# Slot distances on GpSimd instead of ScalarE, and the layer-1 bias of two more chunks in ten written by ScalarE: a graph network kernel on one core

## The chip, the cores and the metric

The kernel runs on one core of one Trainium2 chip. The metric is the time of one execution in device microseconds. The kernel before the change takes 575.55 us (median of three runs, 574.04 to 575.84). Its profiled execution spans 573.7 us, at a mean granted TensorE clock of 0.983.

## The reference, cut to what matters

128 graphs of 64 nodes with 128 features each. For every pair of nodes (i, j) a message is made by a three-layer network with layer norms, multiplied by the adjacency (0 or 1), and summed over j; a second network turns the sum and the node's own features into an update.

```python
def _mlp(x, w0, b0, g0, be0, w1, b1, g1, be1, w2, b2):
    h = relu(x @ w0 + b0);  h = _layernorm(h, g0, be0)
    h = relu(h @ w1 + b1);  h = _layernorm(h, g1, be1)
    return h @ w2 + b2

pair_feats = concatenate([f_i, f_j], axis=-1)             # (B, 64, 64, 256)
messages   = _mlp(pair_feats, msg...) * coupling_matrix[..., None]
agg        = sum(messages, axis=2)
updated    = part_feats + _mlp(concatenate([part_feats, agg], axis=-1), upd...)
```

The adjacency is sparse: each entry is set with a chance of 1/16, made symmetric, with the diagonal. So the kernel computes messages for edges alone.

## The kernel before

The graphs are taken in pairs, 128 nodes on 128 partitions. The edges of a graph get `CAP` = 640 slots, in the order of their node i. 64 pairs make 160 **chunks** of 512 slots (`NCHK`), and every ten chunks (`CPB`) form a block of four pairs, whose adjacency is handled together. The edge-level work is one software pipeline: iteration n runs layer 0 of chunk n and layer 1 of chunk n - 8 (`L1` = `QC` + 3 = 8), with everything else hung into it by a table, `at(iteration, place, function, ...)`. Each engine executes its instructions in the order in which the loop emits them. The places are run as follows.

```python
for n in range(last + 1):
    run(n, "a")
    run(n, "m")
    ...
    if 0 <= n - L1 < NCHK:
        layer1(n - L1)
    run(n, "b")
    if n + LEAD < QC or QC <= n < NCHK:
        layer0(n if n >= QC else n + LEAD)
    if n + 1 < QC or QC <= n - 1 < NCHK - 1:
        stats0(n - 1 if n > QC else n + 1)
    run(n, "k")
    if 0 <= n - L1 < NCHK:
        stats1(n - L1)
    for k in ("x", "x1", "x2", "e0", "e1", "e"):
        run(n, k)
```

**Slots.** Node i of a graph owns the slots from `before` + 1 to `cum`, `deg` of them. `slot` holds 1, 3, 5 ... (twice the slot's number less one), and `mid` = `cum` + `before`, so a slot belongs to the node where |slot - mid| < deg. `distance` writes |slot - mid| for 640 slots, `make_tp` compares it with the degree and gives the matrix `tp` of ones and zeros, from which come the selection matrix of layer 0 (through a cast, `node_rows`, and a DMA), the marks of node j (`marks`) and the weights of the sum.

```python
slot = const.tile([P, CAP], F16, name="slot")
nc.gpsimd.iota(slot, pattern=[[2, CAP]], base=1, ...)

def distance(p):
    b, q = divmod(p, PB)
    D[p] = tpp.tile([P, CAP], F16, name="d", bufs=2)
    nc.scalar.activation(D[p], slot, AF.Abs, bias=blocks[b]["mid"][:, q:q + 1], scale=-1.0)

def make_tp(p):
    b, q = divmod(p, PB)
    tp = tpp.tile([P, CAP], F16, name="tp")
    nc.vector.tensor_scalar(tp, D.pop(p), blocks[b]["deg"][:, q:q + 1], None, op0=ALU.is_lt)
    TP[p] = tp
# ... in the schedule, for p > 2, with n = p * 10 // 4:
at(max(n - 7, p - 2), "a", distance, p)
at(max(n - 6, p - 2), "m", make_tp, p)
at(n - 5, "a", node_rows, p)
```

**Layer 0 and its statistics.** `layer0` makes 512 columns of `hps` in PSUM by matmuls with the selection matrix, and ScalarE turns them into h. `stats0` transposes the four tiles of the chunk before into one bank `hT`, from which VectorE takes mean and variance. GpSimd and ScalarE turn those into a deviation `m_sd` per edge, every five chunks.

**Layer 1 and its bias.** The first layer norm is folded into the next weights, so the layer-1 bias of an edge is `b1b` times the edge's own deviation. There are two ways to put it into the bank `z` before the four matmuls of the chunk add to it. Either ScalarE writes it, four activations of 128x128 (`seed`), or TensorE does, by one matmul with the transposed deviations (`sdT`) as weights. There are two `z` banks, used in turn.

```python
def seed(n):
    q, c = divmod(n, QC)
    z_of(n)
    SEEDED.add(n)
    for t in range(CH):
        k = CH * c + t
        nc.scalar.activation(Z[n][:, t, :], W["b1b"], AF.Copy, scale=SR[q][:, k:k + 1])

def layer1(n):
    q, c = divmod(n, QC)
    ps = z_of(n)
    del Z[n]
    h = H.pop(n)
    if n not in SEEDED:
        nc.tensor.matmul(ps, lhsT=SD[q], rhs=W["b1t"][:, CH * c:CH * c + CH, :],
                         start=True, stop=False, skip_group_check=True)      # line 602
    for t in range(CH):
        nc.tensor.matmul(ps[:, t, :], lhsT=h[:, t * P:(t + 1) * P], rhs=W["w1c"],
                         start=False, stop=True, skip_group_check=True)      # line 605
    Y[n] = yp.tile([P, CH, C], F32, name="y")
    nc.scalar.activation(Y[n], ps, AF.Relu)
# ... in the schedule:
for n in range(2, NCHK - L1):
    if n % CPB in (0, 1, 2, 6, 7, 9):
        at(n + L1 - 2, "x", seed, n)
```

So six of ten chunks are seeded by ScalarE, each in the iteration two before its layer 1, and four (3, 4, 5, 8) get their bias from TensorE.

**GpSimd.** Its work in the loop: `place` and `place_out` (the slots of a block), `node_rows`, the small steps from statistics to variances (`square_sum`, `var1_of`), the low part of the deviations, the weights of the sum, and the residual.

Of the kernel before, what the change touches and what calls it, by code (L numbers as in the profile page):

```python
# [9 lines left out]
F32 = mybir.dt.float32  # L10
# [3 lines left out]
AF = mybir.ActivationFunctionType  # L14
ALU = mybir.AluOpType
AX = mybir.AxisListType
PSUM = bass.MemoryType.PSUM

EPS = 1e-5
BIG = 3.0e38  # L20


@with_exitstack
def tile_gnn(
# [40 lines left out]
    nc = tc.nc  # L65
    B, N, C = x.shape
    P = 128
# [6 lines left out]
    CH = 4  # L74
    QC = QT // CH
    NCHK = NQ * QC
    PB = 4
    NB = NP // PB
    CPB = NCHK // NB
# [57 lines left out]
    eps_c = const.tile([P, 1], F32, name="eps_c")  # L137
    nc.vector.memset(eps_c, EPS)
    eps2_c = const.tile([P, 1], F32, name="eps2_c")
# [18 lines left out]
    slot = const.tile([P, CAP], F16, name="slot")  # L158
# [77 lines left out]
    def add_relu(o, ps, sb):  # L236

        nc.vector._custom_dve(TENSOR_ADD_SAT, out=o, in0=ps, in1=sb, s0=BIG, s1=0.0)

    def square_sum(stp, st, n, name, eng=nc.gpsimd):  # L240

        d = stp.tile([P, n], F32, name=name + "_d")
        s = stp.tile([P, n], F32, name=name + "_s")
        m2 = stp.tile([P, n], F32, name=name)
        eng.tensor_tensor(d, st[:, :, 1], st[:, :, 4], op=ALU.subtract)  # L245
        eng.tensor_tensor(s, st[:, :, 2], st[:, :, 5], op=ALU.add)
        eng.tensor_tensor(d, d, d, op=ALU.mult)
        eng.tensor_scalar(d, d, C / 4.0, None, op0=ALU.mult)
        eng.tensor_tensor(m2, d, s, op=ALU.add)
        return m2  # L250
# [7 lines left out]
    def var1_of(stp, st, m20, n, name, eng=nc.gpsimd):  # L258

        v = stp.tile([P, n], F32, name=name + "_v")  # L260
        eng.tensor_scalar(v, m20, EPS, None, op0=ALU.mult)
        m2 = square_sum(stp, st, n, name, eng)
# [22 lines left out]
    def edge_path(es):  # L285
        blkp = es.enter_context(tc.tile_pool(name="blk", bufs=3))
        adp = es.enter_context(tc.tile_pool(name="adp", bufs=2))
# [36 lines left out]
        def at(n, place, fn, *args):  # L324
            plan.setdefault((n, place), []).append((fn, args))

        def run(n, place):
            for fn, args in plan.pop((n, place), ()):
                fn(*args)

        blocks = {b: {} for b in range(NB)}
        TP, S, H, ST0, V0, SD, SH, Y, ST1, Q, OH, WT, YS, MK, D, IR, JR, SR, Z = ({} for _ in range(19))
# [42 lines left out]
        def place(b):  # L375

            blk = blocks[b]
            cum = cumall[:, b * PB:(b + 1) * PB]
            before = adp.tile([P, PB], F32, name="before")
            nc.gpsimd.tensor_tensor(before, cum, blk["deg"], op=ALU.subtract)  # L380
            blk["mid"] = adp.tile([P, PB], F32, name="mid")
            nc.gpsimd.tensor_tensor(blk["mid"], cum, before, op=ALU.add)
            pos = adp.tile([P, PB, N], F32, name="pos")
            nc.gpsimd.tensor_tensor(pos, blk.pop("rk"),
                                    before.unsqueeze(2).to_broadcast([P, PB, N]), op=ALU.add)
            blk["pos"] = pos
# [88 lines left out]
        def distance(p):  # L475
            b, q = divmod(p, PB)
            D[p] = tpp.tile([P, CAP], F16, name="d", bufs=2)
            nc.scalar.activation(D[p], slot, AF.Abs, bias=blocks[b]["mid"][:, q:q + 1], scale=-1.0)  # L478

        def make_tp(p):  # L480

            b, q = divmod(p, PB)
            tp = tpp.tile([P, CAP], F16, name="tp")
            nc.vector.tensor_scalar(tp, D.pop(p), blocks[b]["deg"][:, q:q + 1], None,  # L484
                                    op0=ALU.is_lt)
            TP[p] = tp

        def node_rows(p):
# [89 lines left out]
        def z_of(n):  # L578

            if n not in Z:  # L580
                Z[n] = zbank(n % 2).rearrange("p (t c) -> p t c", t=CH)
            return Z[n]

        def seed(n):

            q, c = divmod(n, QC)
            z_of(n)
            SEEDED.add(n)  # L590
            for t in range(CH):
                k = CH * c + t
                nc.scalar.activation(Z[n][:, t, :], W["b1b"], AF.Copy, scale=SR[q][:, k:k + 1])  # L593

# [204 lines left out]
        L1 = QC + 3  # L799
# [29 lines left out]
        for b in reversed(range(NB)):  # L829
            o = b * CPB  # L830
            n = o + QC + SC

            if b < NB - 1:
                t = STEADY if b < NB - 3 else LAST[b - NB + 3]
# [32 lines left out]
        for p in range(NP):  # L867
            n = p * TG * 2 // CH
            if p > 1:
                if p > 2:  # L870
# [3 lines that stand above are left out]
                at(n - 4, "a", stack, p, 0, IR)  # L874
                for k in range(2):
                    at(n - 5 + k, "k", marks, p, k)
                    at(n - 5 + k, "k", compare, p, k)
                at(n - 3, "a", stack, p, 1, JR)
            w = p // 2 * QC + QC + L1 + p % 2
            last = p // 2 == NQ - 1  # L880
            at(w - 4, "a", node_marks, p)
            q, h = divmod(p, 2)
            for g in range(2):
                wait = h + 2 if q == NQ - 3 else h + 1 if q == NQ - 2 else 2 + (2 * h + g + 1) // 2
                at(*((NCHK + L1, "b") if last else (q * QC + QC + L1 + wait, "e1")), weights, p, g)
            at(NCHK + L1 + 1 if last else q * QC + SC - (q >= NQ - 3), "x1", reduce, p)
        for q in range(NQ):
            n = q * QC + QC if q else LEAD
# [12 lines left out]
        for n in range(2, NCHK - L1):  # L901
            if n % CPB in (0, 1, 2, 6, 7, 9):
                at(n + L1 - 2, "x", seed, n)

# [12 lines left out]
        degrees(0)  # L919
        place_first()  # L920
        distance(0)
        place_pair(0)
        make_tp(0)
        place_rest()
        bias_rows()
# [25 lines left out]
        compare_here(0, 0)  # L951
        rows_lo(0, 0, 0, 2)
        distance(1)
        layer0(0)
        compare_here(0, 1)
        make_tp(1)
        distance(2)
        bias_parts()
# [89 lines left out]
    with ExitStack() as es:  # L1048
        es.enter_context(tc.manual_schedule())
        flag = edge_path(es)  # L1050
# [160 lines left out]
```

## Time and profile before

| engine | busy, us | share of the span | instructions |
|---|---|---|---|
| TensorE, matmul | 549.3 | 96% | 5303 |
| TensorE, weight load | 515.0 | 90% | 5303 |
| VectorE | 479.8 | 84% | 1944 |
| ScalarE | 476.3 | 83% | 1149 |
| GpSimd | 339.6 | 59% | 898 |

The profile calls TensorE PE, its weight load PEld, VectorE DVE, ScalarE ACT and GpSimd POOL. A row of the groups gives the source line, the engine, the operation, the tiles it writes and reads, its shape and count, then busy time and mean duration in ns, then the engine's idle time just before it. A row of the timeline gives start and length in us, then the same names, and in square brackets how long the engine had been idle and whom it waited for. Neighbouring instructions of one kind are merged into one row with a count. Instructions of ScalarE overlap a little, so the time from one start to the next is shorter than a duration; durations of GpSimd are rough.

The operations that the change touches, by their rows in the groups:

| operation | engine | count | mean, ns |
|---|---|---|---|
| distance `d`, 128x640 float16 | ScalarE | 64 | 823 |
| `make_tp`, 128x640 float16 | VectorE | 64 | 385 |
| seed of `z`, 128x128 | ScalarE | 360 | 371 |
| bias matmul of `z`, 80x512 | TensorE | 70 | 484 |

### The profile page before, as it was taken

What the parts mean: (1) busy time and instruction counts of PE and PEld (TensorE: products, weight loads), DVE (VectorE), ACT (ScalarE), POOL (GpSimd) and SP (SyncE); (2) the same over time, 40 slices, a digit from 0 to 9 for tenths busy, and PEclk for the clock granted to TensorE, in tenths of its full rate; (3) what the DMA queues carried; (4) which work ended last, traced back from release to release, by engine and by line L of the source; (5) the groups of instructions that cost most, each with busy time, mean ns of one, the idle gap of its engine ahead of it and who ended that gap; (6) DMA issues with size and microseconds to landing.
All of it is one profiled execution on the core that took longest, in us unless ns stands there. A gap on an engine that the chain in (4) does not pass through costs nothing. (4 is left out here: it accounts for less than half of the span.)

```text
span 573.7 us, 15753 instructions
## 1 busy us (share of the span) xinstructions
PE 549.3 (96%) x5303; PEld 515.0 (90%) x5303; DVE 479.8 (84%) x1944; ACT 476.3 (83%) x1149; POOL 339.6 (59%) x898
## 2 busy tenths in 40 slices
PE   6899899999999999999999999999999999989894
PEld 4687889999999999999999999999999999979883
DVE  5768788997979899797989889798989979786686
ACT  6788979998988889898888989898888989875434
POOL 3435566665657676575757666565767656545342
PEclk7899999999999999999999999999999999998998
DMA  4464645555465545457574545546475464531201
GB/s 101 102 146 114 133 105 133 101 134 111 103 153 111 134 96 142 113 113 128 125 134 110 138 109 130 105 111 154 102 128 108 125 115 109 114 93 30 35 21 41
DMA packets 90769, 63.21 MB, mean 110 GB/s; under 512 B 57398, under 2 KB 74812, under 8 KB 90684
## 3 DMA queue, kind: packets, MB, share of 16 engines
q1 hardware_dynamic: 90396, 62.03, 49.1%
q8 instruction: 43, 0.70, 0.5%
q14 instruction: 42, 0.34, 0.2%
q10 hardware_dynamic: 288, 0.13, 0.1%
HBM read 6.82 MB, written 4.19 MB: 19 GB/s over the span
## 5 line engine op out<-in xcount | busy, mean ns | idle before, releaser
L548 DVE BATCH_NORM_STATS2 st<-hT 128x6 f32<-128x128 f32 x640 | 141.9, 284 | 36.4 <-PE hT L544 34.8
L605 PE MATMUL z<-w1c,h 128*128 128x128 f32 x1280 | 172.2, 277 | 0.0
L605 PEld LDWEIGHTS z<-w1c,h 128*128 128x128 f32 x1280 | 161.2, 192 | 8.0 <-issue 5.1
L593 ACT ACTIVATE z<-b1b,m_sd 128x128 f32<-128x128 f32 x360 | 133.6, 371 | 8.7
L615 DVE BATCH_NORM_STATS2 st<-y 128x6 f32<-128x128 f32 x640 | 137.5, 277 | 2.7 <-ACT y L608 1.4
L608 ACT ACTIVATE y<-z 128x512 f32<-128x512 f32 x160 | 94.5, 591 | 26.2 <-PE z L605 24.5
L538 ACT ACTIVATE h<-hps,b0c 128x512 f32<-128x512 f32 x160 | 109.4, 684 | 3.6 <-PE hps L535 3.3
L544 PE MATMUL hT<-ident,h 128*128 128x128 f32 x640 | 98.2, 276 | 1.5 <-DVE st L548 1.5
L678 POOL TENSOR_TENSOR w<-oh,m_q 128x320 f32<-128x320 f16 x126 | 91.9, 741 | 9.9 <-PE hT L544 5.3
L535 PE MATMUL hps<-s,abl 128*128 128x512 f32 (+3 forms) x256 | 93.2, 376 | 3.7 <-ACT h L538 2.8
L544 PEld LDWEIGHTS hT<-ident,h 128*128 128x128 f32 x640 | 76.7, 142 | 12.0 <-ACT h L538 1.3
L493 POOL CAST i<-tp 128x640 fp32r<-128x640 f16 x58 | 41.6, 718 | 68.0 <-DVE tp L484 49.1
L535 PE MATMUL hps<-s,abh 128*128 128x512 f32 (+3 forms) x256 | 79.5, 329 | 0.0
L691 PE MATMUL ys<-y,w 128*64 128x128 f32 x1280 | 76.9, 275 | 0.0
L691 PEld LDWEIGHTS ys<-y,w 128*64 128x64 f32 x1280 | 69.2, 137 | 4.2 <-issue 3.6
L245 POOL TENSOR_TENSOR m_d<-st 128x20 f32<-128x20 f32 x62 | 16.3, 263 | 88.4 <-DVE st L548 76.7
L517 DVE TENSOR_TENSOR j<-mk,cmpt 128x320 fp32r<-128x320 f32 x124 | 58.6, 473 | 1.2 <-PE mk L509 1.2
L535 PEld LDWEIGHTS hps<-s,abl 128*128 128x128 f32 x256 | 50.0, 195 | 6.2 <-ACT h L538 4.5
L478 ACT ACTIVATE d<-slot,mid 128x640 f16<-128x640 f16 x64 | 52.7, 823 | 0.0
L535 PEld LDWEIGHTS hps<-s,abh 128*128 128x128 f32 x256 | 50.3, 197 | 0.0
L469 DVE TENSOR_TENSOR abl<-mu,abh 128x512 fp32r<-128x512 f32 (+1 forms) x33 | 22.3, 675 | 31.9 <-ACT abh L463 31.7
L509 PE MATMUL mk<-tp,posall 128*128 128x320 f16 x126 | 38.0, 301 | 1.1 <-DVE tp L484 0.9
(226 smaller groups left out, 978.2 us busy)
## 6 DMA issues: line engine op xcount, KB each, us to landing
s<-i SPq DMA_DIRECT2D x124, 160.0 KB, 2.7
s<-j SPq DMA_DIRECT2D x124, 160.0 KB, 2.6
xn<-in_x_dram SPq DMA_DIRECT2D x15, 256.0 KB, 3.6
out_dram<-uo SPq DMA_DIRECT2D x15, 256.0 KB, 2.4
an<-in_adj_dram SPq DMA_DIRECT2D x16, 128.0 KB, 2.7
oh<-tp SPq DMA_TRANSPOSE x64, 3.6
xn<-in_x_dram SPq DMA_DIRECT2D x2, 128.0 KB
out_dram<-uo SPq DMA_DIRECT2D x2, 128.0 KB, 2.6
```

Of the source, the lines that this page charges most:

```text
L478: nc.scalar.activation(D[p], slot, AF.Abs, bias=blocks[b]["mid"][:, q:q + 1], scale=-1.0)
L517: nc.vector.tensor_tensor(JR[p][:, c], MK.pop((p, k))[:, 0:HC], cmpt[:, c], op=ALU.is_equal)
L535: nc.tensor.matmul(ps[:, c:c + w], lhsT=ab[:, g % 4, :], rhs=s, start=(k == 0), stop=(k == 1))
L538: nc.scalar.activation(H[n], ps, AF.Relu, bias=b0c)
L544: nc.tensor.transpose(ps[:, t, :], H[n][:, t * P:(t + 1) * P], ident)
L548: nc.vector.bn_stats(ST0[q][:, CH * c + t, :], ps[:, t, :])
L593: nc.scalar.activation(Z[n][:, t, :], W["b1b"], AF.Copy, scale=SR[q][:, k:k + 1])
L605: nc.tensor.matmul(ps[:, t, :], lhsT=h[:, t * P:(t + 1) * P], rhs=W["w1c"], start=False, stop=True, skip_group_check=True)
L608: nc.scalar.activation(Y[n], ps, AF.Relu)
L615: nc.vector.bn_stats(ST1[q][:, CH * c + t, :], Y[n][:, t, :])
L678: (nc.vector if p == NP - 2 else nc.gpsimd).tensor_tensor(WT[p][:, :, g, :], OH[p][:, :, g * N:(g + 1) * N], Q[q][:, k:k + TG].unsqueeze(2 ...
L691: nc.tensor.matmul(YS[b][g * N:(g + 1) * N, k, :], lhsT=w[:, t, g, :], rhs=y, start=(t == 0), stop=(t == TG - 1))
```

## The change: what it does and what it is for

**Distances on GpSimd.** From the second block on, `distance` is one GpSimd instruction with two operations, (slot x scale) + shift, written as float16. `scale` is 1 / (2 deg), with deg taken as at least 0.5, and `shift` is 1536 - mid x scale. In float16 the numbers around 1536 are whole, so the result rounds to exactly 1536 where |slot - mid| is below deg, and to another number elsewhere. `make_tp` then asks for equality with the constant 1536 in place of a comparison with the degree of the partition. The block's `place` computes `scale` and `shift` once for its four pairs: two small operations on VectorE and three on GpSimd where there was one. The first block keeps the old way. This frees ScalarE of 60 of its 64 distances.

**More seeds on ScalarE.** From the second block on, chunks 5 and 8 of each block are seeded by ScalarE too, and TensorE's bias matmul for them goes. Their seeds are spread over two iterations: of chunk 5 two tiles in the iteration two before its layer 1, two in the one just before; of chunk 8 three and one. Eight of ten chunks are now seeded, and 3 and 4 keep the matmul.

```diff
+TIE = 1536.0
@@ place(b)
-            blk["mid"] = adp.tile([P, PB], F32, name="mid")
-            nc.gpsimd.tensor_tensor(blk["mid"], cum, before, op=ALU.add)
+            half = adp.tile([P, PB], F32, name="half")
+            nc.vector.tensor_scalar(half, blk["deg"], 0.5, 2.0, op0=ALU.max, op1=ALU.mult)
+            blk["scale"] = adp.tile([P, PB], F32, name="scale")
+            nc.vector.reciprocal(blk["scale"], half)
+            mid = adp.tile([P, PB], F32, name="mid")
+            nc.gpsimd.tensor_tensor(mid, cum, before, op=ALU.add)
+            nc.gpsimd.tensor_tensor(mid, mid, blk["scale"], op=ALU.mult)
+            blk["shift"] = adp.tile([P, PB], F32, name="shift")
+            nc.gpsimd.tensor_scalar(blk["shift"], mid, -1.0, TIE, op0=ALU.mult, op1=ALU.add)
@@ distance(p)
-            nc.scalar.activation(D[p], slot, AF.Abs, bias=blocks[b]["mid"][:, q:q + 1], scale=-1.0)
+            if b == 0:
+                nc.scalar.activation(D[p], slot, AF.Abs, bias=blocks[b]["mid"][:, q:q + 1],
+                                     scale=-1.0)
+                return
+            nc.gpsimd.tensor_scalar(D[p], slot, blocks[b]["scale"][:, q:q + 1],
+                                    blocks[b]["shift"][:, q:q + 1], op0=ALU.mult, op1=ALU.add)
@@ make_tp(p)
-            nc.vector.tensor_scalar(tp, D.pop(p), blocks[b]["deg"][:, q:q + 1], None,
-                                    op0=ALU.is_lt)
+            if b == 0:
+                nc.vector.tensor_scalar(tp, D.pop(p), blocks[b]["deg"][:, q:q + 1], None,
+                                        op0=ALU.is_lt)
+            else:
+                nc.vector.tensor_scalar(tp, D.pop(p), TIE, None, op0=ALU.is_equal)
@@ seed(n)
-        def seed(n):
+        def seed(n, t0=0, t1=CH):
...
-            for t in range(CH):
+            for t in range(t0, t1):
@@ schedule of the seeds
             if n % CPB in (0, 1, 2, 6, 7, 9):
                 at(n + L1 - 2, "x", seed, n)
+            elif n > CPB and n % CPB in {5: 2, 8: 3}:
+                k = {5: 2, 8: 3}[n % CPB]
+                at(n + L1 - 2, "x", seed, n, 0, k)
+                at(n + L1 - 1, "x", seed, n, k, CH)
```

## The prediction, on record before the changed kernel was run

> **What bounds the kernel now.** I read the windows view first: the busy time of each engine in one block of ten chunks from the middle of the run, and in the block before it.
>
> ```profile
> 273.95:306.80 32.85, 32.85 (x331) 31.39 (x329) 28.94 (x120) 29.32 (x72) 21.23 (x58) 1.00 0.58 121
> 241.10:273.95 32.85, 32.85 (x332) 31.40 (x329) 28.94 (x120) 29.32 (x72) 21.21 (x58) 1.00 0.63 121
> ```
>
> The columns are the length of the stretch, then TensorE, weight load, VectorE, ScalarE and GpSimd busy, then the granted clock, the DMA share and GB/s. A block takes 32.85 us and TensorE is busy for all of it, twice in a row. So the bound is TensorE's instruction stream, in order and without a gap; ScalarE has 3.5 us per block to spare, GpSimd 11.6. Two consequences: an instruction taken from TensorE shortens the block by its slot, and any new wait on TensorE lengthens it by the whole wait, since nothing there is idle to absorb it.
>
> Next, the page's groups, for what the change touches:
>
> ```profile
> L593 ACT ACTIVATE z<-b1b,m_sd 128x128 f32<-128x128 f32 x360 | 133.6, 371 | 8.7
> L478 ACT ACTIVATE d<-slot,mid 128x640 f16<-128x640 f16 x64 | 52.7, 823 | 0.0
> ```
>
> Then the timeline, at the two places where the change takes the bias matmul (line 602) away. I name iterations by number modulo ten: an iteration n runs layer 1 of chunk n-8, so chunk 5 of a block is multiplied in iteration 3 and chunk 8 in iteration 6. TensorE and ScalarE from iteration 2 into 3:
>
> ```profile
> 273.35 0.29 PE L535 MATMUL hps<-s,abh 128*128 128x256 f32 x1
> 273.48 0.60 PE L544 MATMUL hT<-ident,h 128*128 128x128 f32 x4
> 273.92 0.30 PE L509 MATMUL mk<-tp,posall 128*128 128x320 f16 x1
> 273.95 0.50 PE L602 MATMUL z<-b1t,sdT 80*128 80x512 f32 x1
> ...
> 271.73 0.68 ACT L773 ACTIVATE usdb<-bu1b,um_sd 128x128 f32<-128x128 f32 x2
> 272.32 0.25 ACT L573 CAST sdT<-ma 80x128 fp32r<-80x128 f32 x1
> 273.19 0.60 ACT L608 ACTIVATE y<-z 128x512 f32<-128x512 f32 x1 [0.63 <-PE z L605]
> 273.69 0.68 ACT L538 ACTIVATE h<-hps,b0c 128x512 f32<-128x512 f32 x1
> 274.27 1.58 ACT L593 ACTIVATE z<-b1b,m_sd 128x128 f32<-128x128 f32 x4
> ```
>
> The reader sees that the bias matmul of chunk 5 starts at 273.95, right behind the marks; its four layer-1 matmuls follow at 274.29, so its slot is 0.34 us. ScalarE starts h at 273.69, as soon as the last hps matmul is out, and its next instruction at 274.27. The other place, iterations 4 to 6:
>
> ```profile
> 281.35 0.70 ACT L538 ACTIVATE h<-hps,b0c 128x512 f32<-128x512 f32 x1
> 282.13 0.58 ACT L741 COPY ysumT<-ma 128x512 f32<-128x512 f32 x1
> 282.61 0.83 ACT L478 ACTIVATE d<-slot,mid 128x640 f16<-128x640 f16 x1
> 283.34 0.30 ACT L269 ACTIVATE m_sq<-m_v,eps_c 128x20 f32<-128x20 f32 x1
> 283.54 0.59 ACT L608 ACTIVATE y<-z 128x512 f32<-128x512 f32 x1
> 284.02 0.69 ACT L538 ACTIVATE h<-hps,b0c 128x512 f32<-128x512 f32 x1
> ...
> 284.22 0.47 PE L602 MATMUL z<-b1t,sdT 80*128 80x512 f32 x1
> ```
>
> Here the layer-1 matmuls follow at 284.53, a slot of 0.31 us. ScalarE runs back to back from 282.13 on.
>
> **What the Trainium skill says.** "ScalarE: Activation LUTs", section "What ACT_TABLE_LOAD costs", gives an activation with one per-partition pointer 280 ns plus 0.833 ns an element, and lets neighbours overlap by some 93 ns. The trace agrees: 823 ns for 640 elements (813 by the page), with the next instruction 0.73 us after its start (282.61 to 283.34). "PSUM — Partial Sum Buffer", section "PSUM bank collisions raise a hardware error", asks that PSUM be guarded by semaphores per bank, not per address. The trace looks like it: two usdb writes, into SBUF, take 0.68 us, a pace of 0.30, but four seeds into one bank take 1.58, a pace of (1.58 - 0.37)/3 = 0.40, as if each waited for the one before. And in iteration 5 the four transposes of hT run from 281.06 to 281.66, the first of them (272 ns) done by 281.34, yet the statistics of the first start at 281.69. I therefore take it that layer 1 of a chunk can't start before the last seed of its bank is written, even where its first quarter was ready long before. "GPSIMD Engine Reference", section "Engine selection", calls one-input operations on GpSimd roughly line rate; the cast of 128x640 float16 at 718 ns agrees. "SBUF — State Buffer", section "Who interferes with whom", has GpSimd and a two-port VectorE operation shut each other out; one make_tp of 1094 ns against a median of 369 may be that.
>
> **The change part by part.** 60 of 64 distances leave ScalarE: four per block, 4 x 0.73 = 2.9 us. They sit in iterations 0, 3, 5 and 8. Eight seeds per block come in: 3 x 0.40 + 0.32 for four, 1.53 us, so 3.1 us for two chunks. ScalarE comes out even, at some 29.5 of 32.85 us. The sum is not the point; the place is.
>
> TensorE: chunks 15, 25 ... 145 and 18, 28 ... 148 lose the bias matmul, 28 in all, worth 0.34 + 0.31 = 0.65 us per block, 14 x 0.65 = 9.1 us. That is the whole possible gain: 575.5 - 9.1 = 566.4.
>
> New wait in iteration 3. Chunk 5's seeds 0 and 1 go into iteration 1, after usdb: ScalarE is there at 272.32 and done with them 0.40 + 0.32 later, 273.04, then sdT (0.16 to the next) until 273.20, so the 0.63 us of idle before y is just filled and h stays at 273.70. Seeds 2 and 3 come after h of iteration 2: 273.70 + 0.57 = 274.27 start, + 0.40 + 0.37 = 275.04 end of the last, + 0.06 for the signal = 275.10. TensorE has nothing between the marks and layer 1, so it is ready at 273.95: it waits 1.15 us to save 0.34. Net + 0.81.
>
> New wait in iteration 6. Chunk 8's seeds 0 to 2 go after h of iteration 4: 281.35 + 0.57 = 281.92, three seeds 2 x 0.40 + 0.32 = 1.13, so 283.05; ysumT 0.48, no distance, m_sq 0.20, y 0.48: h of iteration 5 starts at 284.21 instead of 284.02, and seed 3 ends at 284.21 + 0.57 + 0.37 = 285.15, with the signal 285.21. TensorE is ready at 284.22: it waits 0.99 to save 0.31. Net + 0.68.
>
> GpSimd: four distances per block. No row has two pointer scalars. The trace has a 128x128 multiplication by one pointer scalar at 616 ns (line 648) and a constant one of 128x20 at 258, so a pointer may add some 0.25 us; my estimate is 616 + 512 x 0.83 + 250 = 1.3 us. 5.2 us per block on 21.2 leaves 6 idle. In the GpSimd timeline the four places have room: in iteration 0 it waits 2.4 us for VectorE, in iteration 5 2.6 us; in iterations 3 and 8 it pushes the variance steps back by 1.3 us, which ScalarE wants two iterations later. make_tp on VectorE comes an iteration later too. VectorE's comparison keeps type and size, so its 369 ns; two 128x4 operations per block, about 0.2 us each, lie in its 3.9 us of slack.
>
> Sum: 14 x (0.81 + 0.68) = 14 x 1.49 = 20.9 us. 575.55 + 20.9 = 596.5 us.
>
> **The rivals.** (1) Waits by the seed's own quarter and not by the bank: then matmuls of quarter 0 and 1 start at once, quarter 2 (TensorE there at 274.38) waits for 274.70, quarter 3 for 275.10; layer 1 ends about where it ends now, and chunk 8 behaves alike. Nearly nothing is gained or lost: about 572 to 577. The pace of 0.40 and the statistics' wait speak against it. (2) Seeds in time: if ScalarE, freed of the distances, ran ahead, 566.4. Against it: h can't start before TensorE's hps, whatever ScalarE is spared, and the last seed follows h. (3) GpSimd becomes late: its constant scalar operations of 4 and 20 elements, 223 and 258 ns, differ by 2.2 ns an element; at that slope a distance takes 616 + 512 x 2.2 + 250 = 2.0 us, its block has 29 us of 33, and the deviation chain of iteration 5 starts some 0.7 us late, which delays the transposed deviations on TensorE. The wait in iteration 3 gives it 0.8 us of room, so this would add 0 to 5 us in all. (4) The waits are partly hidden at the start and end, where TensorE idles anyway (the last two of the 14 blocks): 2 or 3 us less.
>
> **Range and chances.** The main term rests on order and on durations that repeat to 10 ns; the open point is whether the bank is the unit of waiting (I give it 0.88) and by how much the restart of TensorE and GpSimd add. Predicted 596.5 us, range 585 to 602. Faster by over 2% 0.05 (even rival 2 stops at 1.6%), within 2% 0.13, slower by over 2% 0.82.
>
> **What would show it.** In the changed trace: line 602 at 42 matmuls; seeds at 472; TensorE waiting for seeds 28 times, about 1.1 us each, in iterations 3 and 6, so 25 to 30 us in the waits; a middle block of about 34.3 us with TensorE busy for some 32.2; distances on GpSimd near 1.3 us; h of iteration 5 about 0.2 us later against y's own matmuls. A block at 32.2 us with no such wait would prove me wrong, as would waits on GpSimd in their place.

## The result, and the profile after

The changed kernel takes 605.39 us (median of four runs, 603.87 to 606.93) against 574.88 us before (four runs, 574.04 to 575.84). The ratio is 1.053, with a 95% interval from 1.0488 to 1.0572. It is slower by 30.5 us, where 21 had been predicted, and lies 3.4 us above the range.

The head of the page, then its groups that answer to those of before:

```profile
span 602.2 us, 15901 instructions
PE 550.9 (91%) x5275; PEld 510.7 (85%) x5275; DVE 484.6 (80%) x1974; ACT 475.1 (79%) x1201; POOL 397.9 (66%) x988
```

```profile
L624 PE MATMUL z<-w1c,h 128*128 128x128 f32 x1280 | 175.5, 280 | 22.6 <-ACT z L612 22.6
L612 ACT ACTIVATE z<-b1b,m_sd 128x128 f32<-128x128 f32 x472 | 173.0, 371 | 10.6
L493 POOL TENSOR_SCALAR d<-slot,scale,shift 128x640 f16<-128x640 f16 x60 | 58.1, 968 | 0.1
L621 PE MATMUL z<-b1t,sdT 80*128 80x512 f32 x42 | 20.2, 480 | 0.0
```

ScalarE's total busy time hardly moved (475.1 against 476.3), as the prediction had it: 112 more seeds, 60 fewer distances. TensorE runs 28 bias matmuls fewer (42), and it now stands idle ahead of the layer-1 matmuls for 22.6 us, waiting for seeds. The same is in the table of waits (engine and tile waiting, for whom; us in total, number of times, longest; at the 28th place, in the last block, TensorE waits 2.83 us for `ysumT` instead):

```profile
PE z L624 <- ACT z L612: 22.6, 27, 1.1
```

And a block of ten chunks, in the windows (the columns are those of the prediction's first fence):

```profile
253.75:288.30 34.55, 32.90 (x329) 31.01 (x326) 29.32 (x121) 29.44 (x76) 25.15 (x63) 1.00 0.51 115
```

A block takes 34.55 us instead of 32.85, and TensorE, busy for all of it before, is idle for 1.65. The two places are the predicted ones. Iteration 2 into 3 in the timeline, ScalarE first and TensorE under it:

```profile
286.66 0.76 ACT L612 ACTIVATE z<-b1b,m_sd 128x128 f32<-128x128 f32 x2
...
288.08 0.68 ACT L557 ACTIVATE h<-hps,b0c 128x512 f32<-128x512 f32 x1
288.65 2.28 ACT L612 ACTIVATE z<-b1b,m_sd 128x128 f32<-128x128 f32 x6
...
288.30 0.30 PE L528 MATMUL mk<-tp,posall 128*128 128x320 f16 x1
289.48 1.16 PE L624 MATMUL z<-w1c,h 128*128 128x128 f32 x8 [0.88 <-ACT z L612]
```

Two seeds of chunk 5 are written from 286.66 on. The other two are the first of the six that start at 288.65, behind h: at a pace of 0.40 us the second of them ends at 288.65 + 0.40 + 0.37 = 289.42. TensorE finishes the marks and then waits until 289.48, although the first quarters had been ready for two microseconds. So layer 1 waits for the last write to the tile `z`; the tile is one bank, and no run here tells bank and tile apart. From the marks to layer 1 it was 0.37 us before and is 1.18 now: + 0.81. Iterations 4 to 6:

```profile
297.22 1.20 ACT L612 ACTIVATE z<-b1b,m_sd 128x128 f32<-128x128 f32 x3
298.35 0.58 ACT L760 COPY ysumT<-ma 128x512 f32<-128x512 f32 x1
298.83 0.31 ACT L270 ACTIVATE m_sq<-m_v,eps_c 128x20 f32<-128x20 f32 x1
299.04 0.58 ACT L627 ACTIVATE y<-z 128x512 f32<-128x512 f32 x1
299.52 0.69 ACT L557 ACTIVATE h<-hps,b0c 128x512 f32<-128x512 f32 x1
300.08 1.07 ACT L612 ACTIVATE z<-b1b,m_sd 128x128 f32<-128x128 f32 x3
...
299.16 0.60 PE L755 MATMUL ma<-ident,uy 128*128 128x128 f32 x4
300.51 1.16 PE L624 MATMUL z<-w1c,h 128*128 128x128 f32 x8 [0.76 <-ACT z L612]
```

The fourth seed of chunk 8 starts at 300.08 and ends 0.37 later, at 300.45; TensorE goes on at 300.51, 0.06 after it. Against the work around it, layer 1 starts 0.69 us later than before.

A second loss lies outside the blocks, at the start. The first layer-1 matmul of the loop starts at 38.89 us, before at 34.80: + 4.1. The span of 28.5 us more is made up of this 4.1, of 23.8 between the first and the last chunk's layer 1 (536.36 us against 512.58), and of 0.6 behind it. The start in the timeline, GpSimd, then ScalarE, then TensorE:

```profile
20.18 0.20 POOL L388 TENSOR_TENSOR mid<-cumall,before 128x4 f32<-128x4 f32 x1
22.66 0.20 POOL L389 TENSOR_TENSOR mid<-mid,scale 128x4 f32<-128x4 f32 x1 [2.28 <-DVE scale L386]
...
25.51 0.88 POOL L493 TENSOR_SCALAR d<-slot,scale,shift 128x640 f16<-128x640 f16 x1
...
29.98 0.31 ACT L256 ACTIVATE m_sd<-m,eps_c 128x20 f32<-128x20 f32 x1 [5.40 <-POOL m L250]
30.45 0.40 ACT L178 ACTIVATE wg<-u,ug1c 128x128 f32<-128x128 f32 x1
...
30.90 0.80 PE L181 MATMUL z<-wg,mean_m 128*128 128x128 f32 x2 [3.14 <-ACT wg L178]
```

It is read as a chain. GpSimd needs the second block's `scale`, and VectorE computes that behind four statistics and a comparison: GpSimd stands for 2.28 us. The position table, the bias table and the first variances (`m`) follow behind it on GpSimd, with a distance in between. So ScalarE waits 5.40 us for `m` (before 1.79), and what stands behind it on ScalarE, `wg` (a folding of weights), comes late too: TensorE waits 3.14 us, where before it had waited 1.59, for an h.

### The profile page after: what moved, and what is told of

Its sections match the earlier page's. It is cut to its first block, busy times and chain, and to the rows that moved or that the text cites. A ratio compares the mean times of both kernels' runs of the same rounds, so it can differ in the third digit from the quotient of the medians.

```text
span 602.2 us, 15901 instructions
## 1 busy us (share of the span) xinstructions
PE 550.9 (91%) x5275; PEld 510.7 (85%) x5275; DVE 484.6 (80%) x1974; ACT 475.1 (79%) x1201; POOL 397.9 (66%) x988
## 5 line engine op out<-in xcount | busy, mean ns | idle before, releaser
L624 PE MATMUL z<-w1c,h 128*128 128x128 f32 x1280 | 175.5, 280 | 22.6 <-ACT z L612 22.6
L624 PEld LDWEIGHTS z<-w1c,h 128*128 128x128 f32 x1280 | 159.4, 192 | 36.9 <-ACT z L612 30.2
L612 ACT ACTIVATE z<-b1b,m_sd 128x128 f32<-128x128 f32 x472 | 173.0, 371 | 10.6
L493 POOL TENSOR_SCALAR d<-slot,scale,shift 128x640 f16<-128x640 f16 x60 | 58.1, 968 | 0.1
L472 ACT CAST abh<-mu 128x512 fp32r<-128x512 f32 (+1 forms) x33 | 18.9, 572 | 45.7 <-PE mu L460 45.7
```

Of the source, the lines that this page charges most:

```text
L493: nc.gpsimd.tensor_scalar(D[p], slot, blocks[b]["scale"][:, q:q + 1], blocks[b]["shift"][:, q:q + 1], op0=ALU.mult, op1=ALU.add)
```

## The experiments

Three theories were on the table. **A**: the 30 us are waits for late seeds, by the bank, in the two places. **B**: a part comes from GpSimd's distances, at the start or in the blocks. **C**: the seeds cost, wherever they are written, because ScalarE has no room. Each ratio is to the kernel before in the same session, where that took 575.6 to 576.3 us. No version leaves out a needed part of the computation.

**The distances alone.** The changed kernel without the new seeds:

```diff
-            elif n > CPB and n % CPB in {5: 2, 8: 3}:
-                k = {5: 2, 8: 3}[n % CPB]
-                at(n + L1 - 2, "x", seed, n, 0, k)
-                at(n + L1 - 1, "x", seed, n, k, CH)
```

> The distances go to GpSimd, the seeds stay as in the kernel before. Theory (the loss in the blocks is TensorE waiting for late seeds, and some 4 us at the start come from GpSimd): no wait of TensorE for seeds, a middle block of 32.85 us again, only the start longer by about 4 us: 579 us. Rival (GpSimd with its 1 us distances, or its sharing with VectorE, slows the pipeline): blocks of 33.5 us or more, 590 to 600 us.

Measured: 581.15 us, ratio 1.0108 (1.0064 to 1.0152), against 575.57. The window of a middle block:

```profile
270.77:303.63 32.86, 32.86 (x331) 31.40 (x329) 29.15 (x120) 27.15 (x68) 25.21 (x63) 1.00 0.57 126
```

The block is that of before, to 0.01 us, with TensorE full; from the first chunk's layer 1 to the last it takes 512.59 us (before 512.58). Of the 4.9 us by which the profiled span grew, 4.6 lie at the start (first layer 1 at 39.36 us instead of 34.80), where ScalarE waits 5.43 us for `m`; the medians are 5.6 apart. In the blocks the distances are off every path; GpSimd has the room that the prediction gave it.

**The seeds alone.** The kernel before with `seed(n, t0, t1)` and the four lines above added.

> The split seeds of the change, with all distances left on ScalarE. Theory: no loss at the start; iteration 3 waits as in the changed kernel, iteration 6 waits 0.73 us longer since the distance of iteration 5 again stands in the ScalarE chain before the last seed: a block of 34.55 + 0.73 = 35.3 us, 575 + 14 x 2.4 = 609 us. Rival (the GpSimd distances cause the loss): 566 to 577 us.

Measured: 611.0 us, 1.059 (1.0539 to 1.0641).

```profile
283.64:318.92 35.28, 32.95 (x329) 31.04 (x327) 28.92 (x118) 31.90 (x80) 21.21 (x57) 1.00 0.56 117
```

```profile
PE z L605 <- ACT z L593: 31.6, 27, 1.8
```

The waits are there without any GpSimd distance, and longer: ScalarE still has a distance ahead of the last seed of chunk 8. A block loses 35.28 - 32.85 = 2.43 us. The changed kernel's 34.55 says that moving the distances gives 0.73 of that back.

**All four seeds in time.** The changed kernel with chunks 5 and 8 seeded in one piece, in the iteration two before their layer 1:

```diff
-            elif n > CPB and n % CPB in {5: 2, 8: 3}:
-                k = {5: 2, 8: 3}[n % CPB]
-                at(n + L1 - 2, "x", seed, n, 0, k)
-                at(n + L1 - 1, "x", seed, n, k, CH)
+            elif n > CPB and n % CPB in (5, 8):
+                at(n + L1 - 2, "x", seed, n)
```

> The change, but all four seeds of chunks 5 and 8 in the iteration two before their layer 1, none in the one just before. Theory (the place of the last seed makes the wait): TensorE waits for no seed any more; instead the four seeds push h back, and the hps matmuls of iterations 3 and 6 wait about 0.4 and 0.3 us for h; a block of about 33.0 us, with the start 581 us. Rival (the load of ScalarE, not the place of the last seed, makes the loss): the same eight seeds per block, so still 34 us or more per block, 600 us.

Measured: 586.55 us, 1.0191 (1.0126 to 1.0255), 5.5 us above the expectation; the block is 33.26 us, with no wait of layer 1 for a seed. So 1.29 of the 1.70 us come from when the last seed is written, and go when the same eight seeds are written earlier. But 33.26 is still more than 32.85, with two bias matmuls fewer.

**The last seeds ahead of h.** The same last part, emitted ahead of layer 0 of its iteration instead of behind it, so that h doesn't stand in front:

```diff
-                at(n + L1 - 1, "x", seed, n, k, CH)
+                at(n + L1 - 1, "b", seed, n, k, CH)
```

> The change, but the last part of the seeds is emitted ahead of h of its iteration, after y, and not behind h. Theory: h (0.57 us) leaves the chain in front of the last seed, so TensorE waits about 0.6 us less in iteration 3 and in iteration 6: waits of some 0.55 and 0.4 us, a block of about 33.4 us, 587 us. Rival (load of ScalarE): no difference, 34.5 us and 604 us.

Measured: 587.59 us, 1.0202 (1.0166 to 1.0239), with a block of 33.40 us.

```profile
PE z L624 <- ACT z L612: 7.0, 27, 0.5
```

The wait falls from 22.6 us to 7.0. It was h, ahead of the last seeds, that made them late.

**Distances on GpSimd from the third block on.** The changed kernel with the second block the old way, which takes `scale`, `shift` and the distance out of the start (`b == 0` becomes `b < 2`, in `place`, `distance` and `make_tp`).

> The change, but the second block too keeps its distances on ScalarE and its plain middle, so that GpSimd takes them over from the third block on. Theory (the 4 us at the start are GpSimd's: it waits 2.3 us for scale from VectorE, then runs the longer place and a distance ahead of the bias table and the first variance): layer 1 of chunk 0 starts at 35 us again instead of 39, and the rest keeps its blocks of 34.55 us: 4 us less than the changed kernel, 601 us. Rival (the start is longer for the larger program or its layout): no difference, 605 us.

Measured: 600.74 us, 1.0414 (1.0355 to 1.0473), with a block of 34.55, and ScalarE's wait for `m` at the start 1.78 us again. It is 24.5 us above its own session's 576.24. The two losses now stand alone, and they add up within the scatter: 24.5 (seeds) + 5.6 (start) = 30.1, where the change costs 30.5. One sign missed: in its profile layer 1 starts at 37.41 us and not at 35, with TensorE's clock at 0.50 from 31 to 34 us. This clock is taken up below.

**Wait or distance at the start?** The changed kernel, with the second block's `scale` and `shift` still computed where they are, and GpSimd still multiplying by them, but that block's distances on ScalarE:

```diff
+            if b == 1:
+                blk["mid"] = mid
+                mid = half
+                nc.gpsimd.tensor_tensor(mid, blk["mid"], blk["scale"], op=ALU.mult)
+            else:
+                nc.gpsimd.tensor_tensor(mid, mid, blk["scale"], op=ALU.mult)
@@ distance, make_tp
-            if b == 0:
+            if b < 2:
```

> The changed kernel with the second block's scale and shift still computed, and GpSimd still multiplying by them ahead of the position table, but that block's four distances on ScalarE again. At the start the changed kernel's first deviation waits 5.4 us for GpSimd instead of 1.8. If GpSimd's wait for VectorE's scale is the cause, that wait stays near 1.8 + 2.3 + 0.4 = 4.5 us and the time near 604 us; if GpSimd's distance itself is the cause, it falls to about 2.7 us and the time to about 602 us.

Measured, in a single run: 608.39 us.

```profile
23.36 0.20 POOL L392 TENSOR_TENSOR half<-mid,scale 128x4 f32<-128x4 f32 x1 [2.20 <-DVE scale L386]
30.23 0.31 ACT L256 ACTIVATE m_sd<-m,eps_c 128x20 f32<-128x20 f32 x1 [4.96 <-POOL m L250]
```

ScalarE's wait stays at 4.96 us of 5.40 without the distance. Of the 3.6 us by which `m` is late in the changed kernel, 2.2 to 2.3 are thus GpSimd's wait for VectorE's `scale`, and the distance is 0.4 to 0.9: its own slot is 0.84 us, but in this run another step, `m_d`, took 0.69 us instead of 0.24. The time of this single run, above both expectations, is no verdict: TensorE's clock was 0.50 from 29 to 46 us.

That clock is a part of the start's cost by itself. The first two windows are of the kernel before and of the changed one, the third is of "the last seeds ahead of h":

```profile
28.00:36.00 8.00, 6.41 (x46) 5.62 (x46) 5.06 (x14) 6.38 (x17) 5.19 (x5) 1.00 0.46 116
```

```profile
28.00:36.00 8.00, 4.53 (x17) 3.77 (x18) 3.10 (x8) 4.48 (x13) 7.07 (x14) 0.57 0.18 42
```

```profile
28.00:30.00 2.00, 1.74 (x5) 0.74 (x4) 1.40 (x5) 0.00 (x0) 1.81 (x5) 0.52 0.59 135
```

In the changed kernel the clock (the seventh figure) is 1.00 until 29.0 us, 0.50 until 35.6, then 1.00 again. "TensorE: Matmul & The Clock Gate", section "What's actually happening", has the clock halved after an idle window of about 3.4 us and restored after as long a busy one. The return agrees here (busy without a gap from 32.3 to 35.6), but not in the run just shown, where TensorE is busy from 33.2 on and the clock returns at 46.2. The fall does not agree: it comes some 1.3 us into the gap of 3.14 us. Nor is the gap shown to be its cause. In the third window the clock is at 0.52 while TensorE is busy for 1.74 of 2.00 us, and the gap of that run begins only at 29.74. All five profiles with the 3.1 us gap have the half clock, and so have three of the eight without it (the seeds alone, GpSimd from the third block on, the deviation moved), after waits of 1.4 and 1.6 us.

These three show what the half clock costs. From one matmul that all profiles share, the one that waits 1.41 us for `abl`, to the first layer 1 they take 10.51 to 10.57 us; the five at full clock take 8.97 to 8.99, the changed kernel 13.54. So, as an estimate from these, 1.5 us of the loss at the start go with the half clock and 3.0 with the chain above (4.5 in all, and 4.1 from the start of the span, as the changed kernel's profile reaches that matmul 0.5 us earlier). Whether the longer wait makes the half clock more likely stays open.

**Why was the block still over 32.85?** Matching TensorE's instructions of "all four seeds in time" one by one with those of the kernel before showed layer 1 of chunk 5 at 0.24 us earlier, as it should be, and then three small steps back: 0.29 us in iteration 3, between layer 1 and the hps matmuls, 0.23 ahead of the transposes of `uy` in iteration 5, and 0.24 ahead of the transposed deviations in iteration 6. The next versions went after these.

*No deviations that nobody reads.* "All four seeds in time", with the second block the old way, and without the transposed deviations (`sh`, its transpose, `sdT`) of the groups of five chunks that are now seeded throughout:

```diff
+        def all_seeded(q):
+            return q % 2 == 1 and CPB < q * QC and (q + 1) * QC <= NCHK - L1
...
+            if all_seeded(q):
+                return
...
+            if not all_seeded(q):
+                at(..., turn_root, q)
+                at(..., root_out, q)
```

> All seeds two iterations ahead, distances on GpSimd from the third block on, and the transposed deviations left out for the groups of five chunks that are seeded throughout (odd groups; nothing reads them there), which takes 0.11 us from TensorE and 0.3 us from ScalarE in iterations 1 and 2. Theory (what is left of the loss is h behind the four seeds): against the 33.26 us block with whole seeds, 0.11 less for the transpose and 0.2 to 0.3 less of wait in iteration 3: a block of 32.9 us, the start as before: 575 us. Rival (GpSimd or another engine bounds the block by now): 33.2 us or more.

Measured: 580.5 us, 1.0087 (1.0061 to 1.0113), with a block of 33.18. It missed by the time, but not by the wait that it named. In "all four seeds in time" the hps matmuls of iteration 3 had waited for h, as their weight load shows:

```profile
283.00 0.19 PEld L554 LDWEIGHTS hps<-s,abl 128*128 128x128 f32 x1 [0.24 <-ACT h L557]
```

This wait is gone: TensorE is 0.36 us ahead of the kernel before up to these hps matmuls. Then it loses 0.33 at the next transposes of hT. VectorE's rows, then TensorE's:

```profile
275.07 0.17 DVE L388 TENSOR_SCALAR half<-deg 128x4 f32<-128x4 f32 x1
275.28 0.18 DVE L390 RECIPROCAL scale<-half 128x4 f32<-128x4 f32 x1
...
277.84 0.66 PE L567 MATMUL hT<-ident,h 128*128 128x128 f32 x4 [0.17 <-DVE st L571]
```

The transposes of hT wait for statistics, and the two operations that the change put on VectorE, 0.33 us to the next start, stand ahead of those: the slack that the prediction counted was the block's, not this place's. One producer's lateness had hidden the next one's.

*The deviation of iteration 5 moved.* The same, with the square root `m_sq` of layer 1's statistics behind h:

```diff
-            at(end + wait, "a", root1_of, q)
-            at(end + wait, "m", inverse_of, q)
+            late = q % 2 == 0 and q < NQ - 3
+            at(end + wait, "x" if late else "a", root1_of, q)
+            at(end + wait, "x" if late else "m", inverse_of, q)
```

> As the kernel without the odd groups' transposes, and the second deviation of iteration 5 (0.2 us on ScalarE) moved from ahead of y to behind h. Theory: h of iteration 5 starts 0.2 us earlier, the wait of the hps matmuls in iteration 6 falls to about 0.1 us: a block of 32.4 to 32.7 us, 568 to 573 us, a little faster than the kernel before. Rival (the block is bounded elsewhere): no gain over the kernel it is made from.

Measured: 580.03 us, 1.0067 (1.0048 to 1.0087), block 33.17. It missed as well: what was moved was not what TensorE waited for. The loss at hT (0.31 us) and the other two steps (0.23 and 0.24) stayed.

*The three places loosened.* The last seed of chunk 8 comes behind `ysumT` (place "a" of the next iteration), the deviation of iteration 6 ahead of y, and `scale` is computed two iterations earlier:

```diff
+                if b > 1:
+                    at(r + 1, "x", scales, b)        # half and scale, on VectorE
...
-            at(*((n, "e1") if last else (n + 1, "b")), root_of, q)
+            early = q % 2 == 0 and 0 < q < NQ - 3
+            at(*((n, "e1") if last else (n + 1, "a" if early else "b")), root_of, q)
...
+            elif n > CPB and n % CPB == 8:
+                at(n + L1 - 2, "x", seed, n, 0, 3)
+                at(n + L1 - 1, "a", seed, n, 3, CH)
```

> From the kernel with the second deviation moved, three edits, each at a wait that its trace shows: scale is computed on VectorE in iteration 9, where it idles, and not in iteration 2 ahead of statistics that TensorE waits for; the last seed of chunk 8 comes behind ysumT at the head of iteration 5, so that the bank of the next transposes is free in time; the deviation of iteration 6 comes ahead of y. Theory (these small waits are all that is left): a block of 32.85 - 0.65 - 0.11 = 32.1 us, at most 32.3, 565 to 568 us: faster than the kernel before by 1.3 to 1.8%. Rival (something else paces the block): 33 us and 578 us.

Measured: 574.92 us, 0.9975 (0.9951 to 0.9998): the first version that isn't slower than before, but far from the expected time. Its block is 32.73 us, a gain of 0.12. Where the rest went is in the timeline, ScalarE's rows, then TensorE's weight load:

```profile
288.84 1.59 ACT L624 ACTIVATE z<-b1b,m_sd 128x128 f32<-128x128 f32 x4
290.36 0.25 ACT L604 CAST sdT<-ma 80x128 fp32r<-80x128 f32 x1
...
290.67 0.42 PEld L451 LDWEIGHTS ma<-ident,xn 128*128 128x128 f32 x4 [0.41 <-ACT sdT L604]
```

The copy `sdT` stands behind four seeds, and the next transposes need the bank that it empties. Against the kernel before, TensorE is 0.46 us ahead just before these transposes and only 0.14 after them. The wait of hT for the statistics and the steps of iterations 5 and 6 are gone in this version, so `scale`, the last seed and the deviation had made them, together at least; they were not varied one by one.

*The same with all distances on ScalarE*, to see what the GpSimd half is worth once the seeds are in time (`if b < 2` becomes `if True`; `scale` and `shift` go):

> The same kernel, but with all distances on ScalarE, as before the change. Theory (the distance of iteration 5, 0.73 us, stands ahead of the last seed of chunk 8 and of h): about 0.5 to 0.7 us more per block than with the distances on GpSimd, 32.7 us, 573 to 577 us, so that the gain hangs on the GpSimd half of the change. Rival (the GpSimd half is worth nothing once the seeds are in time): within 2 us of the kernel with the distances on GpSimd.

Measured: 584.01 us, 1.0135 (1.0106 to 1.0163), well above the expected 573 to 577; the block is 33.38 us, and waits for seeds are back:

```profile
PE z L636 <- ACT z L624: 3.2, 14, 0.6
```

So theory C holds for the seeds without the other half: the GpSimd distances are worth 9 us here, 0.65 in each middle block. Of the two halves of the change this is the one that makes room; it only shows when the seeds use it in time.

*The copy ahead of the seeds.* The loosened version with `sdT` emptied one iteration earlier, ahead of the four seeds:

```diff
-                at(n + 2 if q else QC + 2, "x" if last else "a", root_out, q)
+                at(*((n + 1, "x") if early else (n + 2 if q else QC + 2, "x" if last else "a")), root_out, q)
```

> The loosened version (all seeds in time) has a block of 32.73 us, and the only wait left in it that is as long as what it should have gained is that the first transpose of the next node features waits for ScalarE's copy sdT, which stands behind four seeds in iteration 7: 0.32 us per block. Here that copy is put ahead of those seeds. If this wait is what took the gain back, the block falls to about 32.4 us and the time by 14 x 0.32 = 4.5 us, from 574.9 to about 570.5 us. If TensorE is held there by something else that comes just as late (the rival), the block stays at 32.7 and the time at 574 to 576.

Measured: 572.04 us (20 runs), against 575.65: ratio 0.9937 (0.9916 to 0.9958). Expected were 570.5.

```profile
264.86:297.34 32.48, 32.48 (x328) 30.95 (x326) 28.99 (x120) 28.82 (x74) 24.97 (x62) 1.00 0.61 128
```

This version beats both kernels, the one before by 3.6 us (0.6%) and the changed one by some 33. TensorE is busy for the whole block again, and the block is 0.37 us shorter than before. The 0.25 us that the copy had cost are back. But only eleven of the 14 blocks gain the 0.37, together 4.1 us; the third, 33.22 us against 33.09, and the last, 36.23 against 35.74, lose 0.6. From the first chunk's layer 1 to the last it takes 509.00 us (before 512.58).

What limits it now is again TensorE's own stream, with one step back left, in iteration 3. TensorE's rows, then ScalarE's:

```profile
272.44 0.30 PE L535 MATMUL mk<-tp,posall 128*128 128x320 f16 x1
272.57 1.05 PE L636 MATMUL z<-w1c,h 128*128 128x128 f32 x8
273.50 0.44 PE L561 MATMUL hps<-s,abl 128*128 128x384 f32 x1
...
272.77 0.68 ACT L564 ACTIVATE h<-hps,b0c 128x512 f32<-128x512 f32 x1
```

The hps matmuls follow 0.93 us after the first of layer 1 (before 0.81), 0.05 after h of the iteration before ends at 273.45; that h stands behind four seeds. It looks like the next wait of the same kind, but was not taken away.

These rows also give the true worth of a bias matmul. From the marks to layer 1 it is 0.13 us here and 0.37 before: 0.24 us, not the 0.34 of its slot.

## Why the prediction was too low

**What held.** The direction, the cause and the two places. TensorE waits in iterations 3 and 6 for the last seed of the bank, behind h. The step "it waits 1.15 us to save 0.34", net + 0.81, measured + 0.81 (0.37 to 1.18); net + 0.68 measured + 0.69. That the wait goes by the bank and not by the quarter, to which the prediction gave 0.88, is seen in 289.48: the first quarters were written two microseconds before. The counts of seeds (472) and bias matmuls (42) were as announced, h of iteration 5 came 0.2 us later, and VectorE's comparison with a constant cost no path. Rival 3, GpSimd late in the blocks, falls with "the distances alone": 32.86. Rival 2, seeds in time, did not happen in the changed kernel; it is what the last versions were made into, and even there its 566.4 us was not reached.

**Which steps failed.** The mechanism of the blocks was right; three terms that the sum left at zero were mis-sized. In order of size:

1. *The start*: + 4.1 us in the profile, + 5.6 in the medians of "the distances alone", predicted 0. The step that failed is "GpSimd: the four places have room", read from the timeline of the blocks alone, with "two 128x4 operations lie in VectorE's 3.9 us of slack". The sum held only blocks. In the second block, whose `place` falls into the start, `scale` comes behind VectorE's statistics, and GpSimd holds the first variances behind it: there the path goes GpSimd, ScalarE, TensorE. About 1.5 us of it go with the half clock.

2. *The restart*: 0.10 to 0.11 us at each of the two places in a block, 2.9 us in all, predicted 0 (the prediction named it as open). After the wait the z matmuls of a chunk (eight rows in the profile for the four of the code) take 1.16 us instead of 1.05. It is not the wait as such. The rows of the weight load and of the matmuls, first of the kernel before (chunk 5), then of the changed one (chunk 5), then again of the kernel before:

```profile
274.06 1.09 PEld L605 LDWEIGHTS z<-w1c,h 128*128 128x128 f32 x8
274.29 1.05 PE L605 MATMUL z<-w1c,h 128*128 128x128 f32 x8
...
289.48 0.97 PEld L624 LDWEIGHTS z<-w1c,h 128*128 128x128 f32 x8 [1.19 <-ACT z L612]
...
279.59 0.97 PEld L605 LDWEIGHTS z<-w1c,h 128*128 128x128 f32 x8 [0.17 <-issue]
279.60 1.16 PE L605 MATMUL z<-w1c,h 128*128 128x128 f32 x8
```

   Where the first weight load begins 0.1 to 0.24 us ahead of the matmuls, the eight take 1.05 or 1.06 us in both kernels, with one exception in each; where both begin together they take 1.16. The kernel before has 28 groups of this second kind, none of which waits for a seed. In the changed kernel the waits hold the weight load back as well (the 1.19 us in its row), so its head start is lost. The block sum is 0.81 + 0.69 + 0.22 = 1.72, measured 1.70, predicted 1.49; 14 x 1.70 = 23.8 us instead of 20.9.

3. *The ends*: rival 4 would have taken 2 or 3 us off. Nothing came off: the last block lost 1.6 us like the others, and the end behind it grew by 0.6.

So 20.9 + 2.9 (restart) + 4.1 to 5.6 (start) + 0.6 = 28.5 to 30.0; measured 28.5 in the profiled span and 30.5 in the medians. What stays open of it is under 2 us: two of the four runs were at 604 and two at 607, the latter with a mean TensorE clock of 0.975 instead of 0.982.

**Two signs that read otherwise.** The waits were to sum to 25 to 30 us with TensorE busy for 32.2 us of a block; they sum to 22.6, 27 times, with 32.90 busy. The net loss is the same. The profile counts TensorE idle from the end of its last matmul (0.88 and 0.76 us at the two places), the prediction from the time at which the next could have started (1.15 and 0.99).

**Sizes that were off without harm.** The distance on GpSimd took 0.97 us on average (median 0.87), not 1.3; no row of GpSimd had shown the 0.83 ns an element of that estimate. The whole possible gain was not "9.1 us" but 14 x 2 x 0.24 = 6.7, as a slot is the time between two starts, and layer 1 could not follow the marks or transposes as closely as the bias matmul had. So seeds in time would not have reached 566.4.

## What to carry to other kernels

Where an in-order engine is full, spreading a producer's work over two iterations moves its last part behind whatever that engine does in between: ask when the last write of the bank lands, not how busy the producer is. Work moved to an idle engine costs nothing in steady state and may still cost at the start, where its input stands behind other work and one-off preparation stands behind it; so read the first iterations as a stage of their own. And a slot's length is not its worth: take the start of what follows, with and without, and expect a gain on a full engine to meet the next late producer, as here h, then the statistics, then the copy `sdT`.

## What the hardware showed that was not expected

The four fp32 matmuls of 128x128 of a chunk, eight in the profile, took 1.16 us where the first weight load began together with them, with or without a wait ahead, and 1.05 or 1.06 us where it had begun 0.1 to 0.24 us ahead. Between 28 and 46 us, TensorE's clock was 0.50 for 3.4 to 17 us in eight of the thirteen profiles; in three of these TensorE had waited no longer than 1.6 us at a time in the ten microseconds before, and in one the clock fell while TensorE was busy. And the GpSimd distance, two operations with a pointer scalar each on 128x640 float16, takes 0.87 us (median), hardly more than ScalarE's 0.82 for the same array.
